# Taking softmax's scaling and row extreme in one VectorE operation that moves the scores to SBUF

## The chip, the cores and the metric

The kernel runs on one core of one Trainium2 chip. The core has a matrix engine (TensorE, "PE" in the profile, with its weight loads as "PEld"), VectorE ("DVE"), ScalarE ("ACT"), GpSimd ("POOL") and SyncE ("SP"), which issues most of the DMAs. Each engine works through its own queue in order, and semaphores join the queues. The metric is the device time of one execution, in microseconds; lower is better. All data is fp32.

## What is computed

The reference is a decoder of two layers over x (4 x 512 x 512) and a context of 4 x 512 x 256. Layer 0 is a single-head attention among the context's rows, followed by a linear map whose weights are made from sigmoids of bit planes. Layer 1 is a cross-attention of 16 heads with RMS-normalised queries and keys, followed by a mixture of 16 experts (on batch 0's 512 tokens, four experts each). Each part is added to x behind a tanh gate. The part that matters here is layer 1's attention:

```
q = rmsnorm((layernorm(x) @ Wq) per head, gq)
k = rmsnorm((ctx @ Wk) per head, gk)
v = (ctx @ Wv) per head
scores = q @ k.T / sqrt(128)
out = softmax(scores) @ v        # per batch and head, 512 x 512 scores
x = x + tanh(g) * (out @ Wo)
```

## The kernel before

**Tiling.** Rows go in chunks of 128. Layer 1's 16 heads go in pairs: a group m is a batch and two heads, so there are 4 x 8 = 32 groups and 64 heads. The main loop is `step(i)` over the 64 heads; each step has four quarters, and each quarter does one score tile (128 query rows by 512 keys) and some other work. In all there are 256 score tiles.

**Order.** The program order on every engine is written out by hand: the kernel runs under a manual schedule, and `tick` and `later` keep a counter of matmuls. `later(n, f)` issues f once n more ticks have passed, so what is delayed is placed behind n matmuls' worth of other work in the queues. In a step, the quarters also hold the keys and values of the next group (`keys_values`, L733), the next queries (`queries`, L807), the product of probabilities and values for an earlier head (`values`, L903), the output projection (`project`, L954), and from about 550 to 1300 us the experts' blocks (L1029, L1057), one to a group.

**The softmax of one tile.** `scores(i, c)` writes a tile of raw scores into a PSUM bank, psS (two of these in turn). `top` follows with delay 0: VectorE takes the negated row maximum (nmax, L864), multiplies it by the row's scale rq (sb, L866), and ScalarE reads the bank and makes exp(rq * score + sb) into a tile prob (three in turn), with the row sums in den (L873). The bank is free again when ScalarE has read it. `share` (delay 2) takes the reciprocal of den (L877) and scales prob (L878); `turn` (delay 3) transposes prob in blocks of 32 into tP (L260). After the fourth tile of a head, 16 DMAs from SyncE's queue (L268) put the blocks into place for `values`. The last head of all is turned by TensorE instead (`end_turn`), and its exponential writes its output in another order of columns.

**The scale.** Queries are multiplied by gqk (L189: gq times gk times 128^-0.5) on their way out of PSUM (L815). Their inverse norms, rq, are computed at the side: squares on ScalarE (L813), sums on VectorE and TensorE (L827, L835, L840 to L843), and a power on GpSimd (L192). rq holds one value per query row, head and chunk.

**Keys.** `keys_values` ends with a chain on several queues: squares (L748), sums (L752), a power and a product on GpSimd (L192, L759), four transposes on VectorE (L770), a store of tK to memory issued from ScalarE's queue (L777), and four loads back into kT issued from the same queue (L785).

**The output of a head.** `values` fills a bank psO; ScalarE copies it to oT (L910), in its queue behind whatever stands there; `project` multiplies oT by wo, and VectorE adds the result to x (L275).

Of the kernel before, what the change touches and what calls it, by code (L numbers as in the profile page):

```python
# [11 lines left out]
AF = mybir.ActivationFunctionType  # L12
ALU = mybir.AluOpType
AX = mybir.AxisListType
# [6 lines left out]
D = 128  # L21
# [33 lines left out]
def tile_gated_decoder(  # L55
# [19 lines left out]
    nc = tc.nc  # L75
# [14 lines left out]
    def ps_s():  # L90
        return ps("psS", 2)
# [13 lines left out]
    def row(tag, bufs):  # L105
        return work.tile([P, 512], F32, tag=tag, bufs=bufs, name=tag)

    def col(n, tag):
        return tiny.tile([P, n], F32, tag=tag, name=tag)
# [70 lines left out]
    def sm(name):  # L180
        lo, hi = SMALL[name]
        return small[:, lo:hi]
# [3 lines left out]
    nc.scalar.activation(tg, small[:, 0:4], AF.Tanh)  # L186

    gqk = const.tile([P, 1], F32, name="gqk")
    nc.vector.tensor_scalar(gqk, sm("gq"), sm("gk"), float(D) ** -0.5, ALU.mult, ALU.mult)  # L189

    def rsqrt(out, v, n):
        nc.gpsimd.tensor_tensor(out, v, mhalf[:, :n], ALU.pow)  # L192
# [5 lines left out]
    def later(n, f):  # L198
        heapq.heappush(pending, (clock[0] + n, next(serial), f))

    def tick(n=1):
        clock[0] += n
        while pending and pending[0][0] <= clock[0]:
            heapq.heappop(pending)[2]()
# [52 lines left out]
    def turn_probs(e, tP, c):  # L257


        nc.vector.transpose(tP[:, :, c, :], e.rearrange("p (j r) -> p j r", r=TB))  # L260

    def move_probs(tP):


        pT = work.tile([P, NT, NC, P], F32, tag="big", bufs=2, name="big")
        for g in range(NT):
            for t in range(NT):
                nc.sync.dma_start(  # L268
                    pT[t * TB : (t + 1) * TB, g].rearrange("r j q -> r (j q)"),
                    tP[g * TB : (g + 1) * TB, t * NC : (t + 1) * NC].rearrange("r j c q -> r (j c q)"),  # L270
                )
        return pT
# [578 lines left out]
    def scores(i, c):  # L851


        m, h = divmod(i, G)
        sc = ps_s()
        nc.tensor.matmul(  # L856
            sc, q_of[m][h][:, c * P : (c + 1) * P], k_of[m][:, :, h, :], start=True, stop=True
        )
        st = {}

        def top():
            scale = rq_of[m][:, h * NC + c : h * NC + c + 1]
            nmax = col(1, "nmax")
            nc.vector.tensor_reduce(nmax, sc, AX.X, ALU.max, negate=True)  # L864
            sb = col(1, "sb")
            nc.vector.tensor_tensor(sb, nmax, scale, ALU.mult)  # L866
            st["e"] = row("prob", 3)
            st["den"] = col(1, "den")
            e, x = st["e"], sc
            if i == n_heads - 1:  # L870
                e = e.rearrange("p (k t r) -> p k t r", k=NC, r=TB)
                x = sc.rearrange("p (t k r) -> p k t r", t=NT, r=TB)
            nc.scalar.activation(e, x, AF.Exp, bias=sb, scale=scale, accum_out=st["den"])  # L873

        def share():
            rden = col(1, "rden")
            nc.vector.reciprocal(rden, st["den"])  # L877
            nc.vector.tensor_scalar(st["e"], st["e"], rden, None, ALU.mult)  # L878

        def turn():  # L880
            if i == n_heads - 1:
                ends[c] = st["e"]
                return
            if c == 0:
                turned[i] = work.tile([P, S // TB, NC, TB], F32, tag="tP", bufs=2, name="tP")
            turn_probs(st["e"], turned[i], c)
            if c == NC - 1:
                moved[i] = move_probs(turned.pop(i))

        tick()  # L890
        later(0, top)
        later(2, share)
        later(3, turn)
# [403 lines left out]
```

## Time and profile before

| | us |
|---|---|
| median of three runs | 1465.74 (1463.15 to 1471.24) |
| the profiled execution | 1464.92 |
| its span, first to last instruction | 1462.8 |
| mean granted TensorE clock | 0.993 of full speed |
| the 256 score tiles: matmuls L856 | 262.7 busy on TensorE |
| share, scaling of prob, L878 | 133.1 busy on VectorE (x256) |
| share, reciprocal, L877 | 40.7 busy on VectorE (x256) |
| turn, L260 | 179.1 busy on VectorE (x252) |

The profile is one execution. Its page gives the busy time of each engine, the span in 40 slices, the DMA queues, and the chain of work that ended last, followed back from the last instruction to what released each step. Groups gather the instructions of one line, operation and shape: busy time, mean duration, and the idle time of the engine just ahead of them with what ended it. The views of waits say who waited for whom: total time, number of times, longest. Windows give the busy time of each engine in a stretch, with the number of instructions in brackets, then the granted clock, the DMA engines' share and GB/s. The timeline lists instructions with start and duration, and in brackets the engine's idle time before one and its releaser. Matmul ends are modelled, so a busy TensorE may hold gaps too small to show.

### The profile page before, as it was taken

The numbers are of one execution on the slowest core, as the hardware profiler recorded it, in microseconds if no ns is written. First come the engines' busy times: TensorE is split into PE (matmuls) and PEld (weight loads), VectorE is DVE, ScalarE is ACT, GpSimd is POOL, SyncE is SP. The second block draws the span as 40 slices with busy tenths as digits, with TensorE's granted clock in tenths as the row PEclk, the third lists the DMA queues.
The fourth block names the chain that finished last, engine by engine and source line by source line (L and its number), as shares of the span: only waits on it lengthen the run. The fifth ranks groups of instructions, "written<-read, shape, count | busy, mean of one in ns | idle before, by whom it ended". The sixth has DMA issues, their size and how long they took to land.

```text
span 1462.8 us, 13699 instructions
## 1 busy us (share of the span) xinstructions
PE 1427.7 (98%) x3745; PEld 669.5 (46%) x3745; DVE 962.3 (66%) x2160; ACT 533.4 (36%) x1196; POOL 286.2 (20%) x210
## 2 busy tenths in 40 slices
PE   8999999999999999999999999999999999999898
PEld 4544444444444444444444444444444444444334
DVE  4778766677776776665655565665666556567784
ACT  4642233333443433334233333323433333333331
POOL 1324415323111111111111111111011111102310
PEclk9999999999999999999999999999999999999999
DMA  7424016545544545566556576556556656545642
GB/s 258 168 96 163 1 55 164 149 139 128 138 133 132 143 134 166 157 184 169 176 177 178 159 214 192 145 172 204 170 162 186 183 168 192 167 135 167 180 128 74
DMA packets 155346, 226.89 MB, mean 155 GB/s; under 512 B 24576, under 2 KB 90640, under 8 KB 155264
## 3 DMA queue, kind: packets, MB, share of 16 engines
q1 hardware_dynamic: 127312, 177.86, 41.7%
q10 hardware_dynamic: 23040, 33.56, 7.5%
q0 software_dynamic: 4912, 14.53, 3.5%
q8 instruction: 33, 0.54, 0.2%
q14 instruction: 49, 0.40, 0.1%
HBM read 129.62 MB, written 30.17 MB: 109 GB/s over the span
## 4 chain that ended last, share of the span: by engine, by line
PE 79%; DVE 10%; SPq 4%; ACT 3%; DMA 2%; issue 1%; POOL 0%; ACTq 0%; DVEq 0%; POOLq 0%
PE psA L733 13%; PE psS L856 12%; PE psA L807 12%; PE psO L903 11%; PE psA L954 6%; PE psA L1029 6%; PE psO L954 4%; SPq L268 4%; PE psT L954 3%; PE psA L1057 3%; PE psA L363 2%; DMA big<-tP 2%; ACT prob L873 2%; DVE tP L260 1%; PE psA L691 1%; DVE nmax L864 1%
## 5 line engine op out<-in xcount | busy, mean ns | idle before, releaser
L873 ACT ACTIVATE prob<-psS,sb,rq 128x512 f32<-128x512 f32 x256 | 199.2, 778 | 607.0 <-DVE sb L866 605.5
L856 PE MATMUL psS<-kT,qT 128*128 128x512 f32 x512 | 262.7, 596 | 2.2 <-ACT prob L873 1.1
L733 PE MATMUL psA<-wkv,ctx 128*128 128x512 f32 x512 | 231.9, 592 | 0.0
L807 PE MATMUL psA<-lnT,wq 128*128 128x512 f32 x512 | 231.3, 592 | 0.0
L903 PE MATMUL psO<-big,v 128*128 128x512 f32 x504 | 226.6, 592 | 0.0
L864 DVE TENSOR_REDUCE nmax<-psS 128x1 f32<-128x512 f32 x256 | 172.7, 675 | 30.7 <-PE psS L856 28.9
L877 DVE RECIPROCAL rden<-den 128x1 f32<-128x1 f32 x256 | 40.7, 159 | 224.5 <-ACT prob L873 223.2
L260 DVE STREAM_TRANSPOSE tP<-prob 128x512 f32<-128x512 f32 x252 | 179.1, 711 | 8.4 <-DVE prob L878 0.5
L807 PEld LDWEIGHTS psA<-lnT,wq 128*128 128x128 f32 x512 | 96.7, 190 | 118.6 <-issue 108.1
L903 PEld LDWEIGHTS psO<-big,v 128*128 128x128 f32 x504 | 95.8, 190 | 120.5 <-issue 112.6
L733 PEld LDWEIGHTS psA<-wkv,ctx 128*128 128x128 f32 x512 | 96.4, 190 | 118.8 <-issue 112.3
L192 POOL TENSOR_TENSOR rq<-qss,mhalf 128x8 f32<-128x8 f32 x32 | 53.2, 1661 | 493.5 <-DVE qss L843 493.4
L192 POOL TENSOR_TENSOR rk<-kss,mhalf 128x8 f32<-128x8 f32 x32 | 52.6, 1644 | 443.3 <-DVE rden L877 281.4
L878 DVE TENSOR_SCALAR prob<-prob,rden 128x512 f32<-128x512 f32 x256 | 133.1, 520 | 9.0
L954 PE MATMUL psA<-wo,oT 128*128 128x512 f32 x256 | 124.9, 606 | 11.1 <-ACT oT L910 11.0
L856 PEld LDWEIGHTS psS<-kT,qT 128*128 128x128 f32 x512 | 93.4, 191 | 91.6 <-issue 71.4
L1029 PE MATMUL psA<-gu,xgT 128*128 128x352 f32 x272 | 86.0, 459 | 0.0
L954 PEld LDWEIGHTS psA<-wo,oT 128*128 128x128 f32 x256 | 48.3, 192 | 74.5 <-issue 55.5
L770 DVE STREAM_TRANSPOSE tK<-kn 128x256 f32<-128x256 f32 x128 | 45.4, 412 | 39.1 <-POOL kn L759 39.1
L1029 PEld LDWEIGHTS psA<-gu,xgT 128*128 128x128 f32 x272 | 51.7, 190 | 37.9 <-issue 16.3
L954 PE MATMUL psO<-wo,oT 128*128 128x512 f32 x128 | 66.2, 643 | 0.0
L275 DVE SCALAR_TENSOR_TENSOR x_sb<-psA,tg,x_sb 128x512 f32<-128x512 f32 x80 | 57.9, 724 | 6.7 <-PE psA L691 3.8
(173 smaller groups left out, 1509.4 us busy)
## 6 DMA issues: line engine op xcount, KB each, us to landing
big<-tP SPq DMA_DIRECT2D x1008, 64.0 KB
k_d<-tK ACTq DMA_DIRECT2D x32, 512.0 KB
kT<-k_d ACTq DMA_DIRECT2D x128, 128.0 KB
wq<-in_wq_dram SPq DMA_DIRECT2D x32, 512.0 KB
wo<-in_wo_dram SPq DMA_DIRECT2D x32, 512.0 KB
gu<-in_gate_dram SPq DMA_DIRECT2D x16, 704.0 KB
gu<-in_up_dram SPq DMA_DIRECT2D x16, 704.0 KB
wkv<-in_wk_dram SPq DMA_DIRECT2D x32, 256.0 KB
```

The costliest lines, as they stand in the source:

```text
L192: nc.gpsimd.tensor_tensor(out, v, mhalf[:, :n], ALU.pow)
L260: nc.vector.transpose(tP[:, :, c, :], e.rearrange("p (j r) -> p j r", r=TB))
L268: nc.sync.dma_start(pT[t * TB : (t + 1) * TB, g].rearrange("r j q -> r (j q)"), tP[g * TB : (g + 1) * TB, t * NC : (t + 1) * NC].rearrange ...
L733: nc.tensor.matmul(pp, ctxs[b][:, k, c * P : (c + 1) * P], wkv[:, k, :, :].rearrange("p a n -> p (a n)"), start=(k == 0), stop=(k == CC - 1),)
L807: nc.tensor.matmul(pp, wq[:, k, h * D : (h + 1) * D], lx1[b][:, k, :], start=(k == 0), stop=(k == KC - 1))
L856: nc.tensor.matmul(sc, q_of[m][h][:, c * P : (c + 1) * P], k_of[m][:, :, h, :], start=True, stop=True)
L864: nc.vector.tensor_reduce(nmax, sc, AX.X, ALU.max, negate=True)
L873: nc.scalar.activation(e, x, AF.Exp, bias=sb, scale=scale, accum_out=st["den"])
L878: nc.vector.tensor_scalar(st["e"], st["e"], rden, None, ALU.mult)
L903: nc.tensor.matmul(po, v[:, k, h * D : (h + 1) * D], pT[:, :, k, :], start=(k == 0), stop=(k == NC - 1))
L954: nc.tensor.matmul(pp, oT[:, j, c * P : (c + 1) * P], wo[:, j, :], start=(j == 0), stop=(j == G - 1))
L1029: nc.tensor.matmul(st[a][:, :FF], st["xgT"][:, k * P : (k + 1) * P], st["gu"][:, a, k, :], start=(k == 0), stop=(k == KC - 1),)
```

## The change

gqk gets a minus sign, so that the scores come out negated. In `top`, one VectorE operation reads the bank, multiplies by rq, writes the result to prob in SBUF, and takes the row's minimum as its accumulator output (a column called top). The second operator, a minimum with 3.0e38, leaves the values as they are and names the operator of the accumulator. The exponential then works in place on prob, as exp(top - prob), with an immediate scale of -1 and one column as bias. The reduction, the small product and the columns nmax and sb are gone. The last head's other order of columns moves from the exponential to the VectorE operation. Layer 0's softmax is not touched.

```diff
-    nc.vector.tensor_scalar(gqk, sm("gq"), sm("gk"), float(D) ** -0.5, ALU.mult, ALU.mult)
+    nc.vector.tensor_scalar(gqk, sm("gq"), sm("gk"), -float(D) ** -0.5, ALU.mult, ALU.mult)
...
             scale = rq_of[m][:, h * NC + c : h * NC + c + 1]
-            nmax = col(1, "nmax")
-            nc.vector.tensor_reduce(nmax, sc, AX.X, ALU.max, negate=True)
-            sb = col(1, "sb")
-            nc.vector.tensor_tensor(sb, nmax, scale, ALU.mult)
+
             st["e"] = row("prob", 3)
             st["den"] = col(1, "den")
-            e, x = st["e"], sc
+            e, x, top = st["e"], sc, col(1, "top")
             if i == n_heads - 1:
                 e = e.rearrange("p (k t r) -> p k t r", k=NC, r=TB)
                 x = sc.rearrange("p (t k r) -> p k t r", t=NT, r=TB)
-            nc.scalar.activation(e, x, AF.Exp, bias=sb, scale=scale, accum_out=st["den"])
+            nc.vector.tensor_scalar(e, x, scale, 3.0e38, ALU.mult, ALU.min, accum_out=top)
+            nc.scalar.activation(
+                st["e"], st["e"], AF.Exp, bias=top, scale=-1.0, accum_out=st["den"]
+            )
```

## The prediction

> **What bounds the kernel now.** I read the page first, then each engine's waits, then the groups with shapes kept apart, then the windows, and last the timeline around each TensorE stall.
>
> ```profile
> span 1462.8 us, 13699 instructions
> PE 1427.7 (98%) x3745; PEld 669.5 (46%) x3745; DVE 962.3 (66%) x2160; ACT 533.4 (36%) x1196; POOL 286.2 (20%) x210
> ...
> PE 79%; DVE 10%; SPq 4%; ACT 3%; DMA 2%; issue 1%; POOL 0%; ACTq 0%; DVEq 0%; POOLq 0%
> ```
>
> TensorE is busy for 1427.7 of 1462.8 us and is 79% of the chain that ended last. The change gives it no work and takes none away, so the end can move only through the 35.1 us in which it is idle and through its clock. The waits of TensorE after 205 us, where layer 1 rules, name who holds it:
>
> ```profile
> PE psA L954 <- ACT oT L910: 11.0, 5, 3.5
> ...
> PE psS L856 <- ACT prob L873: 1.1, 1, 1.1
> PE psS L856 <- DMA big<-tP: 1.1, 1, 1.1
> ```
>
> Columns are total us, times, longest. Only the last two are waits for a score bank, and the second of these is misnamed: in the timeline below, its weight load waits for the exponential.
>
> The 11.0 us have four large parts, in the timeline at 245 (2.88 us), 565 (2.20), 1368 (3.55) and 1408 us (2.10). After each the granted clock is 0.50 for 3.4 to 6.8 us (windows of 1 us: 246.9 to 253.7, and three times about 3.4), which costs half of that: 3.4+1.7+1.7+1.7 = 8.5 us. So the four stalls cost 10.7+8.5 = 19.2 us. Each has one chain: the exponential, then on ScalarE's queue the store of tK (L777), its landing, four issues of kT (L785), the squares and qT, one exponential, the copy oT (L910), then `project`.
>
> VectorE is nearer to the bound than 66% says. From 290 to 550 us, where no expert block runs:
>
> ```profile
> 290.00:550.00 260.00, 259.65 (x625) 115.43 (x625) 191.46 (x422) 102.61 (x237) 50.13 (x34) 1.00 0.49 135
> ```
>
> ```profile
> DVE rden L877 <- ACT prob L873: 48.7, 52, 0.9
> DVE nmax L864 <- PE psS L856: 5.9, 8, 1.0
> ```
>
> VectorE is busy 191.5 us and stands 48.7 us more in `share`, waiting for the exponential: a loop that holds it. Only the 5.9 us before nmax are spells in which it has caught up with TensorE. With 59 scores in this window the slack is 5.9/59 = **0.10 us per score**; what a score costs above that, TensorE pays.
>
> **The change, part by part.** These rows carry the prices (last figure before the bar: mean ns of one):
>
> ```profile
> L873 ACT ACTIVATE prob<-psS,sb,rq 128x512 f32<-128x512 f32 x256 | 199.2, 778 | 607.0 <-DVE sb L866 605.5 <-DVE nmax L864 1.5
> L864 DVE TENSOR_REDUCE nmax<-psS 128x1 f32<-128x512 f32 x256 | 172.7, 675 | 30.7 <-PE psS L856 28.9
> L866 DVE TENSOR_TENSOR sb<-nmax,rq 128x1 f32<-128x1 f32 x256 | 48.8, 191 | 12.5 <-POOL rq L192 1.7
> L302 ACT ACTIVATE prob<-psS,nmax 128x512 f32<-128x512 f32 x16 | 11.1, 691 | 26.9 <-DVE nmax L300 26.9
> L337 ACT ACTIVATE x_sb<-x_sb,gm 128x512 f32<-128x512 f32 x16 | 10.7, 712 | 6.4 <-DVE gm L334 6.4
> L1065 DVE COPY y<-psA 128x512 f32<-128x512 f32 x17 | 11.6, 682 | 0.0
> L275 DVE SCALAR_TENSOR_TENSOR x_sb<-psA,tg,x_sb 128x512 f32<-128x512 f32 x80 | 57.9, 724 | 6.7 <-PE psA L691 3.8
> L400 DVE SCALAR_TENSOR_TENSOR w<-pw,em,w 128x512 f32<-128x512 f32 x12 | 13.5, 1123 | 0.0
> ```
>
> *VectorE.* Removed per score: the reduction and the small product; in the timeline the pair takes 0.88 us from start to end (1428.22 to 1429.10). Added: a scaled copy out of PSUM with a minimum as accumulator output. No row shows that form. From below stands the plain copy out of PSUM, 682 ns; from above, the 1123 ns of L400, half speed. Nearest is L275, from PSUM with a per-partition scalar, 724 ns, though with one operand more; I take 700. The Trainium skill, "VectorE: DVE Perf Modes", says in "Two Vector instructions with no wait between them" that an op with an accumulator output is two instructions, the second reading the accumulator, and in "Rules for kernel authors" that ops should not be fused for speed since only their count matters. By this rule the change saves nothing: two instructions before and after. On ScalarE the row of that read is 194 ns, about 0.10 of it under its parent (1429.87 inside 1429.19 to 1429.97). By the rule's count alone the sum is 0; by the rows it is 700 + 90 to 190 = 0.79 to 0.89 against 0.88. I take 0.85: **-0.03 us**, ends -0.09 and +0.45 (half speed plus the read: 1.33).
>
> *ScalarE.* The exponential reads SBUF instead of PSUM and has one per-partition operand (bias) instead of two. L302, with the bias alone, costs 691 from PSUM; L337, bias alone and in place in SBUF, 712. "ScalarE: Activation LUTs" ("What ACT_TABLE_LOAD costs") puts a pointer operand at about 93 ns, and the VectorE page (TRN2 errata) an SBUF source at 224 cycles against 172, 43 ns more at 1.2 GHz, against this change: 778-93+43 = 728. The row shows only 21 ns for the source, so 712 it is: **-0.07 us**. The denominator then comes 0.03+0.07 = 0.10 us earlier per score.
>
> Most of that buys nothing, since TensorE runs without a gap (259.65 of 260). Where it can buy:
>
> 1. *Score banks.* psS is now free after the VectorE operation, not after the exponential. This is the tail's only such stall:
>
> ```profile
> 1416.35 0.68 DVE L864 TENSOR_REDUCE nmax<-psS 128x1 f32<-128x512 f32 x1
> ...
> 1417.33 0.78 ACT L873 ACTIVATE prob<-psS,sb,rq 128x512 f32<-128x512 f32 x1 [4.04 <-DVE sb L866]
> ...
> 1418.24 0.30 PEld L856 LDWEIGHTS psS<-kT,qT 128*128 128x128 f32 x2 [1.93 <-ACT prob L873]
> 1418.25 1.12 PE L856 MATMUL psS<-kT,qT 128*128 128x512 f32 x2 [1.10 <-DMA big<-tP]
> ```
>
> The bank would be free at 1416.35+0.85 = 1417.2, when TensorE falls idle: -1.0 us, and TensorE is busy from there to the last matmuls, so it reaches the end. The like stall at 1361 us (1.15) goes too, but is worth nothing: the stall at 1368 follows, and its end is set by ScalarE's queue.
>
> 2. *The four oT stalls.* The store of tK is issued as an exponential starts (557.74 and 557.75). At that point about three scores lie behind the last spell in which VectorE had caught up (438.53 to 450.88 in a like group): 3 x 0.10 = 0.3 us earlier; the exponential ahead of oT gives 0.07. Four times 0.35 = -1.4 us. The store, its landing and the kT issues themselves stay.
>
> 3. *A wait moved forward.* The scale rq, from GpSimd, was wanted by the small product; now the long operation waits for it, with `share` and `turn` of earlier scores queued behind. Of 32 groups, nmax starts before rq is ready in three (by 1.15, 1.82 and 0.44 us, at 195, 219 and 254), in seven within 0.12 us after it, else 0.5 to 3.7 after. Cost on VectorE at most 0.68+0.68+0.44 = 1.8 us, mostly inside its slack: +0.3.
>
> The minus sign in gqk and the reordering of the last head, now in the VectorE operation, cost nothing: the same instructions run, and prob is written where its last reader (transpose L260, VectorE's own queue) already stands ahead.
>
> Sum: -1.0-1.4+0.3 = -2.1 us. The profiled execution took 1464.9 (span 1462.8 and 2.1 around it), so 1462.8; the median of the three runs lies 0.8 above that execution: **1463.5**.
>
> **Rivals.**
>
> *Slower: the accumulating form runs at half speed.* Per score 1.33-0.88 = +0.45, less 0.07 on ScalarE: +0.38, of which 0.10 is covered. The expert stretch (600 to 1300, 131 scores) is covered by other waits (VectorE waits 47 us for hh there alone). In the rest there are 93+32 = 125 scores: 0.28 x 125 = +35 us, so **1500**. It decides from +0.10 net per score, i.e. from a new pair of 1.05 us; a pair of 1.15 would give about +12. For it: L400's 1123. Against: L400 has two SBUF operands, while L275 with one in PSUM runs at full speed, as would this.
>
> *Faster: the stalls shrink below what lowers the clock.* The 1.1 us stalls show no lower clock, the 2.1 us one does. If VectorE leads by more than 0.35 us at the tK store, two or more stalls lose their slow spell: from -5 us up to the whole -19.2; at half, -9.6 and the 1.0 of the bank: **1455**. Against: most of each chain is the store's flight and the issues.
>
> *Fusion without effect*: pair 0.88 as before, only items 1 and 3: about 1465. This lies inside the forecast's own range.
>
> **How the numbers follow.** A difference of 0.5% (7.3 us) is about what this kernel's measurement tells from none. Forecast with the third rival 62%, own range 1459 to 1470; slower rival in its degrees 19%; faster rival 19%. The range reaches to 1452, most of the faster rival, and to 1480, the mild part of the slower one.
>
> **What would show it.** Right: the new VectorE row near 700 ns with a small accumulator row, the exponential near 712, the score-bank waits gone, the four oT waits a little shorter. Wrong: a VectorE row above 1 us, TensorE idle between 290 and 550, or four half-clock spells become one or many.

## The result and the profile after

The changed kernel takes **1455.3 us** (median of 5 runs, 1453.17 to 1457.36) against 1467.03 us for the kernel before in as many runs (1463.15 to 1471.24). The ratio is 0.9912, with a 95% interval of 0.9894 to 0.9930: 0.9% faster, 12 us where 2 were forecast. The profiled execution of the changed kernel took 1457.03 us. In the runs below, one of e8's 22 executions took 2159.71 us at a granted clock of 0.655 and is left out of its ratio.

The head of its page, with the shares of the chain that ended last:

```profile
span 1454.8 us, 13743 instructions
...
PE 1425.9 (98%) x3745; PEld 669.9 (46%) x3745; DVE 936.0 (64%) x2160; ACT 523.2 (36%) x1196; POOL 285.5 (20%) x210
...
PE 81%; DVE 9%; ACT 3%; DMA 3%; SPq 3%; issue 1%; POOL 0%; ACTq 0%; POOLq 0%
```

TensorE's work is the same 3745 matmuls, and it still bounds the kernel. Its idle time fell from 35.1 us to 1454.8 - 1425.9 = 28.9 us. The groups with shapes kept apart show the new operations:

```profile
L870 DVE TENSOR_SCALAR_CACHE_REDUCE prob<-psS,rq 128x512 f32<-128x512 f32 x256 | 187.7, 734 | 53.2 <-PE psS L856 47.6 <-POOL rq L192 5.0 <-issue 0.2
L871 ACT ACTIVATE prob<-prob,top 128x512 f32<-128x512 f32 x256 | 184.8, 722 | 571.9 <-DVE prob L870 571.9
L870 DVE DVE_READ_ACCUMULATOR prob<-psS,rq 128x1 f32 x256 | 21.1, 82 | 0.0
```

The accumulator is read by an instruction of its own, 82 ns, that lies almost wholly under its parent. At 1397.84 us the operation starts, at 1398.51 the read, and it ends at 1398.59: 0.75 us in place of the pair's 0.88 (medians of the 59 scores from 290 to 550 us: 0.74 and 0.85). TensorE's waits after 205 us, and VectorE's from 290 to 550 us (total us, times, longest):

```profile
PE psA L954 <- ACT oT L910: 5.8, 5, 2.9
PE psT L835 <- DVE part L827: 1.2, 1, 1.2
PE psS L856 <- DVE prob L870: 1.0, 1, 1.0
```

```profile
DVE rden L877 <- ACT prob L871: 46.7, 53, 0.9
DVE prob L870 <- PE psS L856: 10.9, 11, 1.2
```

The oT waits fell from 11.0 to 5.8 us. VectorE's wait for the exponential became shorter (0.94 to 0.88 us each), and its wait for TensorE grew from 5.9 to 10.9 us: it catches up more often, so each score costs less of its round. The pair's 0.13 us and the wait's 0.06 us make **0.19 us per score**. This is the *round*: from the start of VectorE's first operation on a score, through the exponential, to VectorE's reciprocal. Read as one piece, where the reciprocal waits for the exponential (52 scores in this window), its median is 1.81 us before and 1.63 after.

Two windows of the kernel before and the same of the changed one, over the stalls near 565 and 1408 us (after the length: busy time of TensorE, its weight loads, VectorE, ScalarE and GpSimd; then granted clock, DMA share, GB/s):

```profile
560.00:572.00 12.00, 9.80 (x21) 4.25 (x20) 8.00 (x21) 4.15 (x9) 1.63 (x2) 0.86 0.61 191
1400.00:1415.00 15.00, 12.90 (x28) 5.64 (x28) 11.45 (x27) 6.08 (x13) 0.39 (x1) 0.89 0.69 197
```

```profile
560.00:572.00 12.00, 11.58 (x30) 5.01 (x29) 8.21 (x21) 4.18 (x10) 1.59 (x2) 1.00 0.68 212
1400.00:1415.00 15.00, 13.97 (x35) 6.10 (x34) 13.52 (x34) 5.81 (x14) 1.68 (x1) 1.00 0.57 149
```

Before, the clock is lowered in both (0.86 and 0.89 on average); after, it is full: the stalls shrank from 2.20 to 0.42 us and from 2.10 us to nothing, and the half-speed spells behind them went as well.

Where the time came off can be read by comparing the start of the same instruction (the matmul L835, once a group) in the two profiles. The differences: -3.7 us over the two groups around 565 us, -6.0 over those around 1368 and 1408, -0.8 after the last one, -0.6 around the stall at 245 (as long as before, with 3.4 us of half speed behind it in place of 6.8), -1.1 in small gaps elsewhere up to 531 us, +0.3 near 1330; nothing from 600 to 1300 us, where TensorE runs without a gap in both. These sum to -11.9. In layer 0, which the change does not touch, this execution lost 3.9 us (clock 0.64 and 0.68 from 80 to 90 us, full in the execution before), so the spans differ by 8.0. The medians, 11.7 apart, fit the -11.9.

### The profile page after: what moved, and what is told of

Its sections match the earlier page's. It is cut to its first block, busy times and chain, and to the rows that moved or that the text cites. A ratio compares the mean times of both kernels' runs of the same rounds, so it can differ in the third digit from the quotient of the medians.

```text
span 1454.8 us, 13743 instructions
## 1 busy us (share of the span) xinstructions
PE 1425.9 (98%) x3745; PEld 669.9 (46%) x3745; DVE 936.0 (64%) x2160; ACT 523.2 (36%) x1196; POOL 285.5 (20%) x210
## 4 chain that ended last, share of the span: by engine, by line
PE 81%; DVE 9%; ACT 3%; DMA 3%; SPq 3%; issue 1%; POOL 0%; ACTq 0%; POOLq 0%
PE psA L733 14%; PE psS L856 13%; PE psA L807 12%; PE psO L903 12%; PE psA L954 7%; PE psA L1029 6%; PE psO L954 4%; PE psT L954 3%; PE psA L1057 3%; PE psA L363 3%; SPq L268 3%; PE psA L691 1%; DMA big<-tP 1%; ACT prob L871 1%; DVE prob L870 1%; DVE tP L260 1%
## 5 line engine op out<-in xcount | busy, mean ns | idle before, releaser
L871 ACT ACTIVATE prob<-prob,top 128x512 f32<-128x512 f32 x256 | 184.8, 722 | 571.9 <-DVE prob L870 571.9
L870 DVE TENSOR_SCALAR_CACHE_REDUCE prob<-psS,rq 128x512 f32<-128x512 f32 x256 | 187.7, 734 | 53.2 <-PE psS L856 47.6
L878 DVE TENSOR_SCALAR prob<-prob,rden 128x512 f32<-128x512 f32 x256 | 137.3, 536 | 9.0
L954 PE MATMUL psO<-wo,oT 128*128 128x512 f32 x128 | 62.8, 613 | 0.0
```

The costliest lines, as they stand in the source:

```text
L870: nc.vector.tensor_scalar(e, x, scale, 3.0e38, ALU.mult, ALU.min, accum_out=top)
L871: nc.scalar.activation(st["e"], st["e"], AF.Exp, bias=top, scale=-1.0, accum_out=st["den"])
L954: nc.tensor.matmul(pp, oT[:, j, c * P : (c + 1) * P], wo[:, j, :], start=(j == 0), stop=(j == G - 1))
```

## The experiments

Three theories. **A**: VectorE's shorter round per score brings it further ahead, ScalarE's queue ahead of oT is worked off earlier, and the oT stalls and their half-speed spells shrink. **B**: the gain is the score bank, freed by VectorE rather than by the exponential. **C**: it is the shorter exponential on ScalarE. Each run was timed in five rounds against the kernel before on the same chip.

| run | median us | ratio to before | 95% interval |
|---|---|---|---|
| the change | 1455.30 | 0.9912 | 0.9894 to 0.9930 |
| e1 VectorE's part alone | 1457.65 | 0.9938 | 0.9915 to 0.9960 |
| e2 change, product in the path | 1467.50 | 1.0008 | 0.9995 to 1.0022 |
| e3 before, kT loads later | 1483.94 | 1.0120 | 1.0097 to 1.0142 |
| e4 change, kT loads later | 1475.65 | 1.0062 | 1.0039 to 1.0086 |
| e5 before, tK store earlier | 1471.28 | 1.0018 | 1.0007 to 1.0030 |
| e6 change, tK store earlier | 1458.56 | 0.9932 | 0.9915 to 0.9950 |
| e7 change, slower exponential | 1457.46 | 0.9936 | 0.9918 to 0.9954 |
| e8 change, kT loads by GpSimd | 1463.94 | 0.9975 | 0.9968 to 0.9983 |
| e9 change, product beside the path | 1456.31 | 0.9929 | 0.9914 to 0.9944 |
| e10 before, no row maximum | 1445.35 | 0.9842 | 0.9827 to 0.9857 |
| e11 change, kT by GpSimd at the end | 1452.88 | 0.9900 | 0.9884 to 0.9916 |
| e12 change, two products beside it | 1459.90 | 0.9952 | 0.9939 to 0.9965 |

### VectorE's part alone (e1)

The new VectorE operation with its minimum stays; the exponential reads the bank in PSUM as before, with its long duration, and so frees it as late as before. A product on GpSimd once a group makes the negated rq.

```diff
+            nrq_of[m] = col(G * NC, "nrq")
+            nc.gpsimd.tensor_scalar(nrq_of[m], rq_of[m], -1.0, None, ALU.mult)
...
-                st["e"], st["e"], AF.Exp, bias=top, scale=-1.0, accum_out=st["den"]
+                e, x, AF.Exp, bias=top, scale=nrq_of[m][:, h * NC + c : h * NC + c + 1],
+                accum_out=st["den"],
```

> VectorE part alone: the VectorE operation as in the changed kernel, but the exponential still reads the PSUM bank with two per-partition operands (scale -rq, one more small GpSimd product per group), so the bank is free as late as before and ScalarE costs 778 ns as before. Theory A (shorter VectorE loop brings the tK store forward, the oT stalls and their half-clock spells shrink): most of the gain stays, 1456 to 1460 us against about 1466 before (ratio 0.993 to 0.996). Theory B (score banks freed earlier): nothing left, 1464 to 1467. Theory C (the shorter exponential drains ScalarE's queue): nothing left, 1464 to 1467.

1457.65 us: most of the gain is there without an earlier bank and with an exponential of 778 ns. What B and C add to the time is not told apart from nothing: the intervals overlap. (The traces show one place where B acts; see item 1 below.)

### The shorter round given back (e2)

The changed kernel with one small product on VectorE between the minimum and the exponential.

```diff
+            sb = col(1, "sb")
+            nc.vector.tensor_tensor(sb, top, ones[:, 0:1], ALU.mult)
...
-                st["e"], st["e"], AF.Exp, bias=top, scale=-1.0, accum_out=st["den"]
+                st["e"], st["e"], AF.Exp, bias=sb, scale=-1.0, accum_out=st["den"]
```

> The changed kernel with one small VectorE product put back between the minimum and the exponential (about 0.19 us per score), early bank and short exponential kept. Theory A: the VectorE loop is as long as before, the gain is gone, 1463 to 1468 (ratio 0.998 to 1.002). Theories B and C: 1454 to 1458 as in the changed kernel (ratio about 0.992).

1467.5 us, no different from before: 0.19 us per score put back takes the whole gain, though the bank is still freed by VectorE and the exponential still takes 722 ns. TensorE's waits of e2 ahead of `project` stand in two rows, as the profile names no releaser for one of the stalls:

```profile
PE psA L956 <- ACT oT L912: 8.5, 4, 4.8
PE psA L956 <- issue: 3.4, 1, 3.4
```

Together 11.9 us, as before the change (11.0). Against B and C, for A.

### The link in ScalarE's queue (e3 to e6)

The prediction named the store of tK and the four issues of its loads as the chain ahead of oT. First the loads were put behind the copy oT, in the kernel before (e3) and in the changed one (e4):

```diff
-        later(18, take_in)
+        later(18 if m < 2 else 26, take_in)
```

> The kernel before with only the issues of the kT loads put behind the oT copy in ScalarE's queue, in the groups without an expert block. Theory A, with the stalls at the four oT copies as the place of the gain: the stalls and their slow clock go without any change to the softmax, 1448 to 1455 (ratio 0.988 to 0.993). Theories B and C: the gain has another place, 1463 to 1468; and if kT then comes too late for the next scores, slower than before.

> The changed kernel with the same move of the kT issues. Theory A: what the change gained was in these stalls, so it ends within 3 us of the kernel before with the same move, at 1446 to 1452 (ratio 0.986 to 0.991). Theories B and C: the full 11 us between the two stay.

A's expectation was missed: both became slower, 1483.94 and 1475.65 us. What came true is the clause that stood under B and C, kT too late for the next scores. TensorE's waits in e3:

```profile
PE psS L856 <- DMA kT<-k_d: 22.1, 12, 3.8
PE psS L856 <- DMA big<-tP: 5.7, 1, 5.7
PE psA L954 <- ACT oT L910: 2.2, 2, 1.1
```

The issues did hold oT (11.0 to 2.2 us), but the same loads are then late for the next group's scores, at 12 places. The two kernels stay 8.3 us apart, where A expected at most 3 and B and C expected 11. Their waits for kT are alike (22.1 us in e3, 23.0 in e4); what differs is the other waits after 205 us, 9.8 us in e3 and 1.5 in e4, and the largest of these, the 5.7, stands where e4 waits 4.7 us for kT. This pair does not decide between the theories.

Then the store was issued one exponential earlier, in the kernel before (e5) and the changed one (e6):

```diff
-        later(14, put_out)
+        later(14 if m < 2 else 11, put_out)
```

> The kernel before with only the store of tK issued one exponential earlier in ScalarE's queue, as soon as tK is transposed (some 1.4 us earlier at the stall of 565 us: tK is ready at 556.3, the store was issued at 557.75); the softmax is untouched, the kT loads keep their place. Theory A (what the change bought is an earlier store): about the gain of the change, 1452 to 1459 (ratio 0.991 to 0.996). Theories B and C (banks, shorter exponential): no gain, 1464 to 1468.

> The changed kernel with the same earlier store. Theory A: two stalls at oT are left in it (2.9 and 2.1 us, with 5 us of slow clock in all), and an earlier store takes at least one: 1446 to 1453 (ratio 0.986 to 0.991), the fastest so far. Theories B and C: 1454 to 1457, as the changed kernel.

No gain: 1471.28 us, a small loss (the interval lies above 1), and 1458.56. The oT waits grew, from 11.0 to 14.6 us in e5 and from 5.8 to 9.9 in e6. The timeline of e5 near 565 us says why at this stall:

```profile
562.67 0.34 ACTq L777 DMA_DIRECT2D k_d<-tK  x1
...
567.24 0.78 ACT L873 ACTIVATE prob<-psS,sb,rq 128x512 f32<-128x512 f32 x1 [1.20 <-DVE sb L866]
567.30 0.79 ACTq L785 DMA_DIRECT2D kT<-k_d  x2
```

The loads' issue comes 4.63 us after the store, though it came 3.38 after it in the kernel before (557.75, 561.13). It stands behind an exponential that waits for VectorE. In the old order the loads' issue (561.13) also comes just behind the start of that exponential (560.88), so moving the store alone does not bring it forward: A in the narrow form "the store is the link" falls. In this timeline the link is VectorE's progress through *both* exponentials.

### A slower exponential (e7)

The immediate scale became a column of -1 (neg), which lengthens the exponential from 722 to 813 ns.

```diff
-                st["e"], st["e"], AF.Exp, bias=top, scale=-1.0, accum_out=st["den"]
+                st["e"], st["e"], AF.Exp, bias=top, scale=neg, accum_out=st["den"]
```

> The changed kernel with the exponential's scale as a per-partition column of -1 instead of an immediate: ScalarE pays about 0.09 us more per score (row near 810 ns), nothing else changes. Theory A, in which the whole VectorE loop counts, the wait for the exponential in it too: the loop loses 0.09 of the 0.19 us gained per score, so about half of the gain: 1458 to 1462 (ratio 0.994 to 0.998). Theory B: no change against the changed kernel, 1454 to 1457. Theory C: the gain is gone, 1464 to 1467.

1457.46 us, about 2 above the changed kernel and the intervals overlap; C is out. A's proportional form (0.09 of 0.19 us is half the gain) is missed too: the gain does not follow the round's length in a straight line.

### The loads from another queue (e8, e11)

GpSimd's queue issues the kT loads, in all groups of index 2 and above (e8, 22 runs), or in the last two alone (e11).

```diff
-                nc.scalar.dma_start(
+                (nc.scalar if m < 2 else nc.gpsimd).dma_start(
```

> The changed kernel with the kT loads issued from GpSimd's queue, so that ScalarE's queue no longer stands still for them (3.3 us before sq in the changed kernel's timeline). Theory A with ScalarE's standstill as the last link: the oT stalls go, and the time falls to 1446 to 1452, unless kT arrives later than the next group's scores need it; then a wait of TensorE for kT shows and the time is 1455 or more. Theories B and C: 1454 to 1457.

1463.94 us. TensorE's waits:

```profile
PE psS L856 <- DMA kT<-k_d: 14.7, 3, 7.3
...
PE psA L954 <- ACT oT L910: 0.2, 1, 0.2
```

The oT waits are gone; the loads are late in three places. In the two long ones (5.97 and 7.27 us, at 256 and 578) GpSimd's queue issues them behind its indirect loads. In the last two groups it gains 3 to 4 us over the changed kernel, so only those were moved in e11:

```diff
-                nc.scalar.dma_start(
+                (nc.gpsimd if m >= M - 2 else nc.scalar).dma_start(
```

> The changed kernel with the kT loads of the last two groups alone issued by GpSimd's queue, where no indirect loads stand ahead of them. If ScalarE's queue of kT issues is what remains of the stall at 1368 (2.1 us and its half-speed spell), this stall goes: 1450 to 1454, 1 to 5 us under the changed kernel. If the store's flight sets it by itself, kT comes as late as before and TensorE waits for it instead: no change, 1455 to 1458.

1452.88 us, as expected. The window from 1360 us, first of the changed kernel, then of e11:

```profile
1360.00:1375.00 15.00, 12.88 (x28) 5.60 (x27) 11.75 (x27) 3.98 (x9) 4.96 (x5) 0.89 0.73 209
```

```profile
1360.00:1375.00 15.00, 14.38 (x35) 6.23 (x35) 12.64 (x28) 5.30 (x15) 7.03 (x8) 1.00 0.77 211
```

The stall of 2.12 us shrank to 0.62 and its half-speed spell went. That is the fastest of these kernels that keep the row maximum; against the change alone (0.9900 and 0.9912) the intervals overlap, so a gain of some 2 us is likely, not shown.

### Busy time or round trip? (e9, e12)

The product of e2 lengthens both VectorE's busy time and the round VectorE, exponential, VectorE. In e9 nothing reads its result, so it lies inside VectorE's wait for the exponential; e12 adds a second that reads the first. The cut shows e12; e9 has its first two lines.

```diff
+            sb = col(1, "sb")
+            nc.vector.tensor_tensor(sb, ones[:, 1:2], ones[:, 0:1], ALU.mult)
+            sb2 = col(1, "sb2")
+            nc.vector.tensor_tensor(sb2, sb, ones[:, 0:1], ALU.mult)
```

> The changed kernel with one small VectorE product more per score (about 0.19 us), as in the run with the product in the exponential's path, but here nothing reads its result, so the exponential does not wait for it. It stands ahead of the row that waits for the exponential. Theory A in the form 'the round trip VectorE - exponential - VectorE sets the pace': the product lies inside VectorE's wait for the denominator (46.7 us in 290 to 550), so the time stays at 1455 to 1458, with the wait before the reciprocal down to about 0.7 us each. Theory A in the form 'VectorE's busy time sets the pace': 1463 to 1468, as in the run with the product in the path. Theory B (banks freed earlier) and C (ScalarE): no change from 1455 to 1458.

> The run with the product beside the exponential's path occupied VectorE by only 20.2 us more than the changed kernel (936.0 to 956.2), since the product overlaps the reading of the accumulator; in the path it was 43.1 us (979.1). Here a second product follows, which reads the first, so that both together occupy VectorE by about 0.25 us per score, more than the one in the path, and still nothing waits for them; they fit into VectorE's wait of 0.88 us for the exponential. If VectorE's round trip through the exponential sets the pace: 1455 to 1460. If its busy time does: 1467 or more, busy time near 1000 us.

1456.31 and 1459.9 us, the second at the edge of what was expected. In e9 the product occupies VectorE by only 20.2 us more (956.2 against 936.0 in the changed kernel), so e12 is the stronger test. The heads of the pages of e2 and of e12:

```profile
PE 1430.0 (98%) x3745; PEld 671.0 (46%) x3745; DVE 979.1 (67%) x2416; ACT 518.9 (35%) x1196; POOL 286.2 (20%) x210
```

```profile
PE 1425.4 (98%) x3745; PEld 669.0 (46%) x3745; DVE 1001.1 (69%) x2672; ACT 523.0 (36%) x1196; POOL 285.7 (20%) x210
```

VectorE is busy 22 us longer in e12 than in e2, yet the kernel is 7.6 us faster (ratios 0.9952 and 1.0008, the intervals apart). In the path, 43.1 us of VectorE cost 12.2; beside it, 65.1 us cost 4.6. From 290 to 550 us VectorE's wait took the products in:

```profile
DVE rden L881 <- ACT prob L871: 32.0, 52, 0.6
```

It was 46.7 us in 53 waits. The round, measured as above (medians from 290 to 550 us), beside the times:

| run | round, us | ratio to before |
|---|---|---|
| before | 1.81 | 1 |
| e2 | 1.82 | 1.0008 |
| e7 | 1.72 | 0.9936 |
| e1 | 1.68 | 0.9938 |
| the change | 1.63 | 0.9912 |
| e9 | 1.63 | 0.9929 |
| e12 | 1.63 | 0.9952 |

With the product in the path, e2 has the round and the time of the kernel before; every run with a shorter round is faster. So the round trip sets the pace before busy time does. It is not all: e12 has the changed kernel's round and is 4.6 us slower, its interval apart from the change's. That busy time counts at the scores where VectorE has other work instead of that wait is likely, not shown.

### How far it goes (e10)

The kernel before without the row maximum: no reduction, no product.

```diff
-            nmax = col(1, "nmax")
-            nc.vector.tensor_reduce(nmax, sc, AX.X, ALU.max, negate=True)
-            sb = col(1, "sb")
-            nc.vector.tensor_tensor(sb, nmax, scale, ALU.mult)
...
-            nc.scalar.activation(e, x, AF.Exp, bias=sb, scale=scale, accum_out=st["den"])
+            nc.scalar.activation(e, x, AF.Exp, scale=scale, accum_out=st["den"])
```

> The kernel before with the row maximum left out: no reduction and no small product, the exponential takes rq times the score from PSUM without a bias. VectorE's round per score is shorter by about 0.9 us instead of the change's 0.19. If the oT stalls go with VectorE's progress (A), they should nearly vanish and the half-speed spells with them: 1443 to 1450, oT waits under 3 us. If from some point the chain of the tK store, its landing and the kT issues sets the end by itself (A with a floor), the gain stops near that of the change: 1450 to 1458, oT waits of 4 to 6 us as in the changed kernel. B and C: B expects the banks to be freed earlier too, hence 1455 to 1458 and no more than the change; C expects no gain, as the exponential is not shorter by more than 0.09 us.

1445.35 us, ratio 0.9842. TensorE's waits after 205 us, all of them:

```profile
PE psS L856 <- DMA big<-tP: 2.4, 1, 2.4
PE psT L835 <- DVE part L827: 0.3, 1, 0.3
```

No oT wait is left. The four issues still take 2.53 us of ScalarE's queue near 245 us; with VectorE 0.88 us per score shorter they come early enough. The stalls have no floor of their own in the store and the issues. The run takes away more than a piece of the round, though: its exponential starts on the scores themselves and waits for no VectorE operation.

## Why the prediction was right and wrong

- **The bound**: right. TensorE's waits for oT and the clock behind them held what could be won.
- **VectorE's pair**: 0.75 us against 0.85 forecast and 0.88 before. The operation, 734 ns, was put at 700; the read, 82 ns, costs some 0.02 after its parent, where ScalarE's row gave 0.09 to 0.19. The row taken for the read was of another engine. The rule weighed there, that an accumulator's output is a second instruction, holds in the count (256 reads), but the second one costs next to nothing; "don't fuse" would have given 0, the trace gives -0.13. The slower rival, half speed, did not occur.
- **The exponential**: 722 ns; 712 forecast, 728 by the estimate from the Trainium skill's pages named there. Den comes 0.19 us earlier per score, not 0.10.
- **Item 2, the step that failed**: "about three scores lie behind the last spell in which VectorE had caught up", 3 x 0.10 + 0.07 = 0.35 us for each stall. The view shown there had the better number: 8 such spells in 59 scores, one in 7.4, and 7.4 x 0.19 = 1.4 us. Both factors of the term were too small, the gain per score (0.10 for 0.19) and the number of scores. Measured from the tK store to TensorE's arrival at `project`, the lead grew at the four stalls from 4.97 to 5.80, 7.56 to 8.98, 7.19 to 8.05 and 7.47 to about 8.5 us: by 0.8 to 1.4. That was the condition that the prediction gave its own faster rival, "if VectorE leads by more than 0.35 us", and it happened with the rival's effect: two stalls lost their slow spell, and 1455 was its time. The mechanism was right, its size was too small by a factor of two to four. That the effect is VectorE's round is shown by e2 and e12, and e10 goes the same way. The chain's words "the store, its landing" were too narrow (e5).
- **Item 1, the score bank**: right in its mechanism and size, -1.0 forecast, 0.95 measured at that place (from L835 to the scores that need the bank, 5.80 to 4.85 us). But the sign "the score-bank waits gone" did not come: a wait of 1.03 us stays. The timeline of the changed kernel there, and below it e1, where the exponential still frees the bank:

```profile
1407.19 1.88 PE L856 MATMUL psS<-kT,qT 128*128 128x512 f32 x4
...
1407.56 1.68 POOL L192 TENSOR_TENSOR rq<-qss,mhalf 128x8 f32<-128x8 f32 x1 [14.01 <-DVE qss L843]
...
1408.64 0.73 DVE L275 SCALAR_TENSOR_TENSOR x_sb<-psO,tg,x_sb 128x512 f32<-128x512 f32 x1
1409.30 0.74 DVE L870 TENSOR_SCALAR_CACHE_REDUCE prob<-psS,rq 128x512 f32<-128x512 f32 x1
...
1410.10 1.13 PE L856 MATMUL psS<-kT,qT 128*128 128x512 f32 x2 [1.03 <-DVE prob L870]
```

```profile
1408.28 1.12 PE L859 MATMUL psS<-kT,qT 128*128 128x512 f32 x2 [2.17 <-ACT prob L874]
```

  From VectorE's operation on the bank to the matmuls that reuse it are 0.80 us (1409.30 to 1410.10), where there were 1.89 before (1416.35 to 1418.25): the forecast's 1.0. The wait stays because TensorE now comes to the bank sooner. In the kernel before, the matmuls ahead still ran at half speed (0.48 us for the pair of L835, 0.30 after; from L835 to the first of these scores 2.81 us, 1.94 after), and VectorE is no sooner: its operation comes 3.90 us behind L835 before and 4.05 after, behind an output addition in its own queue, with rq ready just before it (1409.24). In e1 the wait is 2.17 us, so the early bank is worth 1.1 us at this one place.
- **Item 3, the wait for rq moved forward**: it is real, 5.0 us of VectorE in three waits (1.11, 1.76 and 2.14), in the three groups that the prediction named, against the 0.3 to 1.8 weighed. None of TensorE's waits is put down to it.
- **The range** held the time, with luck in it. The forecast's own part, 1459 to 1470, did not hold it, and the value of 1463.5 is 8 us off (its last sum slips too: 1462.8 and 0.8 make 1463.6). The time lies in the part from 1452 that was added for the faster rival, which had 19%. The forecast of no change that a measurement can tell failed.

## What to carry to other kernels

Where an engine that is not the bound runs a loop through another engine, price a change by what it takes off the whole round, and multiply by the number of rounds since that engine last waited for the bound: read that number from its waits, as rounds divided by such waits. (Here this was read off afterwards; it gave 1.4 us where 0.8 to 1.4 were measured, and no second change was forecast with it.) A stall of about 2 us or more can be worth more than its own time, because 3.4 us or more at half speed may follow, so ask what small lead would carry it below. Work beside a loop's path, inside its wait, is nearly free; the same work in the path is not.

## What the runs showed of the hardware

The length of a stall does not alone decide whether the clock halves. In the changed kernel 2.12 and 2.91 us of idle TensorE were followed by half speed; in e11 2.79 us and in e4 2.83 us were not:

```profile
248.50 1.13 PE L954 MATMUL psA<-wo,oT 128*128 128x512 f32 x2 [2.79 <-issue]
```

```profile
295.23 1.10 PE L856 MATMUL psS<-kT,qT 128*128 128x512 f32 x2 [2.83 <-DMA kT<-k_d]
```

In e11 two matmuls take 1.13 us there, the full-speed time, and the granted clock stays 1.00 in every window up to 262 us. But 1.84 us (e2, at 571) and 2.05 (e9, at 1366) were followed by half speed. From 1.84 to 2.83 us it went both ways; below that, 1.76 and 1.62 us left the clock at 1.00 (e2 at 1415, e9 at 356).

Where the stall lies decides most of it. In windows of 0.02 us the clock of the kernel before falls at 246.85, 567.70, 1373.25 and 1410.80 us, which are 94, 236 and 11 times 3.413 us apart. In the other traces with more than one fall the distances are whole multiples of the same 3.413 us too (327 in the changed kernel, 94 and 235 in e2), and each half-speed spell within a kernel's span lasts one, two or three such steps (3.4, 6.8 or 10.2 us). So each execution can be cut into steps that end where its clock falls or could fall, and what counts is the idle time inside one step. The 2.83 us of e4 lie across two steps, with 1.57 and 1.27 us idle; the 1.84 us of e2 lie in one step, and the next has half speed (the granted clock is the third figure from the end):

```profile
290.55:293.96 3.41, 1.84 (x5) 0.54 (x4) 3.01 (x8) 0.05 (x1) 1.84 (x2) 1.00 0.86 220
293.96:297.37 3.41, 2.14 (x5) 1.06 (x6) 0.76 (x2) 0.12 (x1) 0.87 (x1) 1.00 0.46 106
```

```profile
568.60:572.01 3.41, 1.57 (x6) 0.61 (x5) 2.76 (x5) 2.27 (x5) 0.00 (x0) 1.00 1.03 260
572.01:575.42 3.41, 3.41 (x7) 1.52 (x6) 2.39 (x9) 0.81 (x2) 1.37 (x2) 0.50 0.32 119
```

In the thirteen traces where a fall before the kernel's end fixes the steps (all but e11), half speed followed each of the 23 full-speed steps after 195 us with 2.02 us idle or more and none with less than 1.84; in between, two fell and four did not, which stays open. The Trainium skill, "TensorE: Matmul & The Clock Gate" ("Part 1: The HAM clock gate"), has the clock fall after an idle window of about 3.4 us that runs free of the kernel. The traces agree with the free-running window and its length, but the window need not be idle throughout: some 2 us of its 3.4 were enough.

The four issues of the kT loads took 2.38 us before and 4.24 after at the same stall (near 245 us). From the store to the end of these issues are 7.17 us before and 8.03 after, which uses up the 0.8 us by which the lead grew, and the stall did not shrink. There SyncE issues a row of transfers and GpSimd a row of indirect loads at the same time; that these slow the issues was not tried by itself.
